# Message passing over 200,000 edges: rows of x @ W1[:64] gathered from a node table, both tables computed among the first twelve groups, 54 node updates

## The chip, the cores and the metric

The kernel runs on one core of one Trainium2 chip. The metric is the device time of one execution, in microseconds (us). A span is the time from the first to the last instruction of a profiled execution.

## The reference, cut to what matters

```python
# x: (12500, 64) nodes; src, dst: (200000,) with dst sorted; edge: (200000, 32)
msg_in = concatenate([x[src], x[dst], edge], axis=-1)          # 160 columns
messages = relu(msg_in @ mW1 + mb1) @ mW2 + mb2                # mW1 (160,128), mW2 (128,64)
aggregated = segment_sum(messages, dst, num_segments=12500)
upd_in = concatenate([x, aggregated], axis=-1)
out = layernorm(x + relu(upd_in @ uW1 + ub1) @ uW2 + ub2)      # per node, 64 columns
```

`src` is random, `dst` is sorted and dense at low nodes (nodes go as the square of a uniform number), so an early group of edges covers few nodes and a late one many.

## The kernel before, in words

The edges stand in 1563 tiles of 128. Eight tiles are a group, called `s` (`SUB`, 196 groups); sixteen are a supergroup `g` (`SUP`, 98). All work is written in a fixed order (`tc.manual_schedule()`), so each engine executes its instructions in the order of the loop over `s` at the end; a queue never overtakes.

For one group:

- `gather` (L148): POOL issues one indirect DMA for each tile; each brings 128 rows of x (64 columns, 256 bytes) chosen by `src`. Groups are gathered five ahead (`AHEAD`) into seven buffers.
- `transpose` (L268) turns pairs of tiles on PE, and ACT copies the result to `xt` (L272).
- `hidden` sums in PSUM the product of `xt` with W1[:64] (L290) and the product of the operand `l` with `rhs` (L294). The operand `l` holds the edge features and a selection of one of 32 nodes (a window) per edge; `rhs` holds W1[128:] and, for each tile, the 32 rows of the destination table B = x @ W1[64:128] + b1 that the tile can meet. ACT applies the relu (L298).
- `collect` (L309, L310) multiplies the hidden rows with a selection of slots, and also counts edges; `aggregate` (L322) adds eight windows of 32 columns to `comb` on DVE, at column offsets read from `wint`.

For one supergroup: `load` has SP bring `l` (edge features L235, and relative destinations broadcast over 32 partitions L236) and sixteen windows of B (L243); `select` on DVE turns destinations into selections (L252, L254), ACT casts them (L258). One supergroup later a node update follows: `columns`, `update`, `residual` and `norm` compute 384 nodes (L335 to L373) and SP writes them.

Before the loop, x transposed is loaded into `comb` (L88), B is computed in 25 chunks of 512 nodes (L222, L224) and written to DRAM by ACT's queue (L225); destinations less their tile's first destination are computed in bulk (L162 to L197), written to DRAM (`drow`) and checked: where the edges do not fit windows, a general path after L410 runs instead; these inputs do not take it.

SP and ACT issue their own DMAs, and POOL issues the gathers. Each DMA of SP or ACT waits, besides for its data, for the landing of the eighth DMA before it on the two queues together, in program order.

Of the kernel before, what the change touches and what calls it, by code (L numbers as in the profile page):

```python
# [17 lines left out]
P = 128  # L18
# [15 lines left out]
PADDST = -100000  # L34
EK, SK = 0, DE
AHEAD = 5
NCH = 4
UB = 3
NCOL = (-(-N // P) + UB) * P
ONE = 32  # L40
# [3 lines left out]
def gnn_kernel(ctx: ExitStack, tc: tile.TileContext, xT, x, one, eT, e_rows, src, dst, dst_row, wrow,  # L44
               mW1, mb1, mW2, mb2, uW1, ub1, uW2, ub2, out):

# [20 lines left out]

    B = dram.tile([NPAD, DH], F32, name="tab_b")
    drow = dram.tile([1, EBULK], F32, name="drow")


    src_s = const.tile([P, NT], I32, name="src_s")
    nc.scalar.dma_start(src_s[:, :64], src[:, :64])
    nc.scalar.dma_start(src_s[:, 64:], src[:, 64:])
    wint = const.tile([1, NTP], I32, name="wint")
    nc.sync.dma_start(wint, wrow)


    BF = mybir.dt.bfloat16
    w1b = const.tile([P, DH], F32, name="w1b")  # L80
    nc.sync.dma_start(w1b[D:], mW1[D:2 * D, :])
    b1 = const.tile([P, DH], F32, name="b1")
    nc.sync.dma_start(b1, mb1.rearrange("(o f) -> o f", o=1).broadcast_to([P, DH]))

    comb = const.tile([P, 2, NCOL], F32, name="comb")
    XCH = 2048
    for c in range(0, NCOL, XCH):
        nc.sync.dma_start(comb[D:, 1, c:min(c + XCH, NCOL)], xT[:, c:min(c + XCH, NCOL)])  # L88
    rhs = [const.tile([P, SUP // 2, DH], F32, name=f"rhs{k}") for k in range(2)]
    w1a = const.tile([P, DH], F32, name="w1a")  # L90
    for o in (0, 64):
        nc.scalar.dma_start(w1a[o:o + D], mW1[0:D, :])
    w2 = const.tile([DH, D], F32, name="w2")
    nc.scalar.dma_start(w2, mW2)
    b2c = const.tile([D, 1], F32, name="b2c")
    nc.scalar.dma_start(b2c, mb2.rearrange("(f o) -> f o", o=1))
    u1a = const.tile([D, DH], F32, name="u1a")
    nc.scalar.dma_start(u1a, uW1[D:2 * D, :])

    uz = const.tile([P, DH], F32, name="uz")  # L100
    nc.vector.memset(uz[:D], 0.0)
    nc.scalar.dma_start(uz[D:], uW1[0:D, :])
    ub1_s = const.tile([DH, 1], F32, name="ub1_s")
    nc.scalar.dma_start(ub1_s, ub1.rearrange("(f o) -> f o", o=1))
    u2 = const.tile([DH, D], F32, name="u2")
    nc.scalar.dma_start(u2, uW2)

    ux = const.tile([P, D], F32, name="ux")
    nc.vector.memset(ux[:D], 0.0)
    nc.scalar.dma_start(ux[ONE:ONE + 1], ub2.rearrange("(o f) -> o f", o=1))  # L110
    for r in rhs:
        for o in (EK, EK + 64):
            nc.scalar.dma_start(r[o:o + DE], mW1[2 * D:, :].unsqueeze(1).broadcast_to([DE, SUP // 2, DH]))

    ident = const.tile([P, P], F32, name="ident")
    make_identity(nc, ident)
    nc.vector.tensor_copy(ux[D:], ident[D:, D:])
    eps = const.tile([P, 1], F32, name="eps")
    nc.vector.memset(eps, EPS)
    ones = const.tile([P, 1], F32, name="ones")  # L120
    nc.vector.memset(ones, 1.0)
    slot_i = const.tile([P, WIN], I32, name="slot_i")
    nc.gpsimd.iota(slot_i, pattern=[[1, WIN]], base=0, channel_multiplier=0)
    pidx_i = const.tile([P, 1], I32, name="pidx_i")
    nc.gpsimd.iota(pidx_i, pattern=[[0, 1]], base=-SK, channel_multiplier=1)
    nc.gpsimd.iota(pidx_i[64:], pattern=[[0, 1]], base=-SK, channel_multiplier=1)

    cpool = ctx.enter_context(tc.tile_pool(name="cpsum", bufs=1, space=bass.MemoryType.PSUM))
    cps = cpool.tile([P, WIN + 1], F32, name="cps")
    nc.vector.tensor_copy(cps[:, :WIN], slot_i)  # L130
    nc.vector.tensor_copy(cps[:, WIN:], pidx_i)
    slot, pidx = cps[:, :WIN], cps[:, WIN:]
    w2u = const.tile([DH, DH], F32, name="w2u")

    one0 = const.tile([P, P], BF, name="one0")
    nc.vector.memset(one0, 0.0)
    nc.vector.memset(one0[:, 0:1], 1.0)

    rows = ctx.enter_context(tc.tile_pool(name="rows", bufs=AHEAD + 2))
# [5 lines left out]
    def gather(s):  # L145
        a = rows.tile([P, SUB, D], F32, name="xg")
        for i, t in enumerate(tiles(s)):
            nc.gpsimd.indirect_dma_start(  # L148
                out=a[:, i, :], out_offset=None, in_=x[:, :],
                in_offset=bass.IndirectOffsetOnAxis(ap=src_s[:, t:t + 1], axis=0))  # L150
        xg[s] = a

    for s in range(min(AHEAD, NSUB)):
        gather(s)


    drc = const.tile([P, NT], F32, name="drc")
    flag_i = const.tile([1, 1], I32, name="flag_i")
    usup = const.tile([1, NSUP], I32, name="usup")
    with tc.tile_pool(name="bulk", bufs=1) as bulk:  # L160
        dall = bulk.tile([P, TPP, P], I32, name="dall")
        nc.sync.dma_start(dall.rearrange("p t e -> p (t e)"), dst_row.rearrange("o (p c) -> (o p) c", p=P))  # L162
        wbc = bulk.tile([P, NT], I32, name="wbc")
        nc.scalar.dma_start(wbc, wrow[:, :NT].broadcast_to([P, NT]))
        dst_s = bulk.tile([P, NT], I32, name="dst_s")
        nc.scalar.dma_start(dst_s, dst)
        drel = bulk.tile([P, TPP, P], F32, name="drel")
        nc.vector.tensor_tensor(drel, dall, dall[:, :, 0:1].broadcast_to([P, TPP, P]), op=ALU.subtract)
        nc.sync.dma_start(drow.rearrange("o (p c) -> (o p) c", p=P), drel.rearrange("p t e -> p (t e)"))
        nc.vector.tensor_tensor(drc, dst_s, wbc, op=ALU.subtract)  # L170

        far = bulk.tile([P, TPP * P], F32, name="far")
        nc.vector.tensor_scalar(far, drel.rearrange("p t e -> p (t e)"), (WIN - 1) / 2.0, None, op0=ALU.subtract)
        nc.vector.tensor_tensor(far, far, far, op=ALU.mult)
        nc.vector.tensor_scalar(far, far, WIN * WIN / 4.0, None, op0=ALU.is_gt)
        nfar = bulk.tile([P, 1], F32, name="nfar")
        nc.vector.tensor_reduce(nfar, far, AX.X, ALU.add)
        pf = psum.tile([1, 1], F32, name="pf", tag="pt", bufs=1)
        nc.tensor.matmul(pf, nfar, ones, start=True, stop=True)

        wf = bulk.tile([1, NT], F32, name="wf")
        nc.vector.tensor_copy(wf, wint[:, :NT])
        back = bulk.tile([1, NT], F32, name="back")
        nc.vector.tensor_tensor(back[:, 1:], wf[:, 1:], wf[:, :-1], op=ALU.is_lt)
        nc.vector.tensor_copy(back[:, 0:1], pf)
        nc.vector.memset(usup[:, 0:1], 0)
        nc.vector.tensor_copy(usup[:, 1:], wint.rearrange("o (g t) -> o g t", t=SUP)[:, 1:, 0])
        uf = bulk.tile([1, NSUP + 1], F32, name="uf")
        nc.vector.tensor_copy(uf[:, :NSUP], usup)
        nc.vector.memset(uf[:, NSUP:], float(N - WIN))  # L190
        gap = bulk.tile([1, NSUP], F32, name="gap")
        nc.vector.tensor_tensor(gap, uf[:, 1:], uf[:, :-1], op=ALU.subtract)
        nc.vector.tensor_scalar(gap, gap, float(UB * P - WIN), None, op0=ALU.is_gt)
        bad = bulk.tile([1, 2], F32, name="bad")
        nc.vector.tensor_reduce(bad[:, 0:1], back, AX.X, ALU.add)
        nc.vector.tensor_reduce(bad[:, 1:], gap, AX.X, ALU.add)
        nc.vector.tensor_scalar(flag_i, bad[:, 0:1], bad[:, 1:], float((-E) % P), op0=ALU.add, op1=ALU.subtract)  # L197


    with tc.tile_pool(name="sup", bufs=2) as sup, tc.tile_pool(name="work", bufs=2) as work:  # L200
        L, S, SB, xs, hs, pht = {}, {}, {}, {}, {}, {}


        nc.vector.memset(comb[:, 0], 0.0)
        nc.vector.memset(comb[:D, 1], 0.0)
        nc.sync.dma_start(comb[ONE:ONE + 1, 1, :], one)
        pw = psum.tile([D, DH], F32, name="pw", tag="pt", bufs=1)
        nc.tensor.transpose(pw, w2, ident)
        w2T = work.tile([D, DH], F32, name="w2T", bufs=1)
        nc.vector.tensor_copy(w2T, pw)  # L210
        pw2 = psum.tile([DH, DH], F32, name="pw2", tag="pt", bufs=1)
        nc.tensor.matmul(pw2, w2T, u1a, start=True, stop=True)
        nc.vector.tensor_copy(w2u, pw2)
        pw3 = psum.tile([1, DH], F32, name="pw3", tag="pt", bufs=1)
        nc.tensor.matmul(pw3, b2c, u1a, start=True, stop=True)
        nc.vector.tensor_copy(uz[0:1, :], pw3)
        Bv = B.rearrange("(c p) f -> p c f", p=P)
        for c in range(0, NB, NCH):
            n = min(NCH, NB - c)
            pb = psum.tile([P, NCH, DH], F32, name="pb", tag="pc")  # L220
            for i in range(n):
                nc.tensor.matmul(pb[:, i, :], comb[D:, 1, (c + i) * P:(c + i + 1) * P], w1b[D:], start=True, stop=True)  # L222
# [152 lines left out]
        with tc.manual_schedule():  # L375
# [3 lines left out]
            for s in range(NSUB):  # L379
                g, j = divmod(s, SUP // SUB)  # L380
                if s + AHEAD < NSUB:
                    gather(s + AHEAD)
# [185 lines left out]
```

## Time and profile before

| | us |
|---|---|
| runs of the kernel before | 2006.89 median of 3 (2006.82 to 2007.45) |
| profiled execution, own time | 2007.04 |
| profiled execution, span | 2005.3 |
| POOL busy | 1481.1 (74% of the span) |
| PE busy, PE weight load busy | 1576.4 (79%), 1367.2 (68%) |
| DVE busy, ACT busy | 868.8 (43%), 493.0 (25%) |
| granted TensorE clock, mean | 0.789 |

In a list of instructions the columns are start, duration, engine, line and operation, the written tile and what is read, and in square brackets the idle time of the engine ahead of it with what ended it; "issue" means that nothing the profile shows ended it. PE is the matrix engine's product, PEld its weight load. A line of the table of stretches gives the stretch, its length, busy time with the number of instructions of PE, PEld, DVE, ACT and POOL, then the granted clock, the busy share of the DMA engines and GB/s.

### The profile page before, as it was taken

The numbers are of one execution on the slowest core, as the hardware profiler recorded it, in microseconds if no ns is written. First come the engines' busy times: TensorE is split into PE (matmuls) and PEld (weight loads), VectorE is DVE, ScalarE is ACT, GpSimd is POOL, SyncE is SP. The second block draws the span as 40 slices with busy tenths as digits, with TensorE's granted clock in tenths as the row PEclk, the third lists the DMA queues.
The fourth block names the chain that finished last, engine by engine and source line by source line (L and its number), as shares of the span: only waits on it lengthen the run. The fifth ranks groups of instructions, "written<-read, shape, count | busy, mean of one in ns | idle before, by whom it ended". The sixth has DMA issues, their size and how long they took to land.

```text
span 2005.3 us, 39767 instructions
## 1 busy us (share of the span) xinstructions
PE 1576.4 (79%) x12127; PEld 1367.2 (68%) x12127; DVE 868.8 (43%) x2894; ACT 493.0 (25%) x788; POOL 1481.1 (74%) x1572
## 2 busy tenths in 40 slices
PE   1999878877787778877778778778787877788787
PEld 0888766766676667666667667667676766677675
DVE  7356534343434343434443444344434444343443
ACT  0033322222222222222222222222222222222221
POOL 7767777777777777777777777777777777777771
PEclk9999777788777777777877787777777777877776
DMA  7634333333333333333332333333333333333330
GB/s 189 166 90 98 88 76 66 78 66 77 70 74 73 72 70 73 73 71 76 68 75 68 76 68 76 67 77 67 77 67 77 67 78 68 75 68 75 67 77 17
DMA packets 243690, 155.35 MB, mean 77 GB/s; under 512 B 96900, under 2 KB 211108, under 8 KB 243093
## 3 DMA queue, kind: packets, MB, share of 16 engines
q1 hardware_dynamic: 178020, 91.92, 18.7%
q0 software_dynamic: 50016, 51.32, 13.6%
q10 hardware_dynamic: 15442, 9.55, 1.8%
q8 instruction: 101, 1.65, 0.3%
q14 instruction: 111, 0.91, 0.2%
HBM read 135.65 MB, written 16.91 MB: 76 GB/s over the span
## 4 chain that ended last, share of the span: by engine, by line
POOL 44%; issue 20%; PE 18%; DMA 15%; SPq 1%; DVE 1%; POOLq 0%; ACT 0%; ACTq 0%; DVEq 0%
POOL xg L148 44%; DMA xg<-in_x,src_s 13%; PE ph L309 4%; PE pc L290 3%; PE pc L294 3%; PE pu L342 2%; PE pb L222 2%; PE pt L268 1%; PE pu L343 1%; DMA dall<-in_dst_row 1%; SPq L243 1%; PE py L353 1%; PE py L354 0%; DMA comb<-in_xT 0%; DMA rhs<-in_mW 0%
## 5 line engine op out<-in xcount | busy, mean ns | idle before, releaser
L148 POOL DMA_INDIRECT xg<-in_x,src_s x1563 | 1480.1, 947 | 483.8 <-issue 436.4
L322 DVE TENSOR_TENSOR comb<-comb,ph 128x64 f32 x1563 | 346.5, 222 | 592.0 <-PE pt L268 378.0
L268 PE MATMUL pt<-ident,xg 128*128 128x128 f32 x781 | 204.4, 324 | 360.8 <-DMA xg<-in_x,src_s 358.4
L290 PE MATMUL pc<-w1a,xt 64*128 64x128 f32 x3126 | 463.3, 381 | 1.5
L294 PE MATMUL pc<-rhs,l 64*128 64x128 f32 x3126 | 441.5, 366 | 7.8 <-issue 4.6
L309 PEld LDWEIGHTS ph<-sel,h 128*128 128x128 f32 x3126 | 401.3, 204 | 28.5 <-issue 4.5
L268 PEld LDWEIGHTS pt<-ident,xg 128*128 128x128 f32 x781 | 113.7, 156 | 425.3 <-issue 355.3
L309 PE MATMUL ph<-sel,h 128*128 128x32 f32 x3126 | 399.0, 284 | 0.1
L290 PEld LDWEIGHTS pc<-w1a,xt 64*128 64x128 f32 x3126 | 365.1, 275 | 37.7 <-issue 29.1
L294 PEld LDWEIGHTS pc<-rhs,l 64*128 64x128 f32 x3126 | 373.8, 279 | 9.7 <-issue 4.8
L298 ACT ACTIVATE h<-pc 128x1024 f32<-128x1024 f32 (+1 forms) x197 | 200.0, 1016 | 474.8 <-PE pc L294 421.3
L272 ACT COPY xt<-pt 128x512 f32<-128x512 f32 x196 | 114.3, 583 | 744.8 <-PE pt L268 732.2
L358 DVE BATCH_NORM_STATS2 st<-py 128x6 f32<-128x64 f32 x294 | 48.5, 221 | 470.7 <-PE py L354 452.7
L252 DVE TENSOR_TENSOR l<-l,cps 32x1024 f32<-32x1024 f32 x196 | 239.2, 1220 | 27.3 <-DMA l<-drow 20.9
L353 PE MATMUL py<-ux,xw 128*128 128x64 f32 x588 | 136.3, 319 | 0.7 <-ACT hTu L345 0.7
L354 PE MATMUL py<-u,hTu 128*128 128x64 f32 x588 | 129.1, 306 | 0.0
L342 PE MATMUL pu<-comb,w2u 128*128 x196 | 122.4, 716 | 7.3 <-DVE o L371 7.3
L353 PEld LDWEIGHTS py<-ux,xw 128*128 128x128 f32 x588 | 105.4, 224 | 17.2 <-issue 8.2
L354 PEld LDWEIGHTS py<-u,hTu 128*128 128x128 f32 x588 | 104.8, 223 | 0.0
L343 PE MATMUL pu<-xw,uz 128*128 128x384 f32 x196 | 85.8, 521 | 0.0
L371 DVE TENSOR_SCALAR o<-py,mv,rs 128x64 f32<-128x64 f32 x294 | 83.1, 338 | 3.6
L343 PEld LDWEIGHTS pu<-xw,uz 128*128 128x128 f32 x196 | 46.4, 237 | 40.0 <-issue 25.4
(67 smaller groups left out, 594.5 us busy)
## 6 DMA issues: line engine op xcount, KB each, us to landing
l<-in_eT SPq DMA_DIRECT2D x196, 128.0 KB
l<-drow SPq DMA_DIRECT2D x196, 128.0 KB
xg<-in_x,src_s POOLq DMA_INDIRECT x1563
rhs<-tab_b SPq DMA_DIRECT2D x1563, 16.0 KB
out<-o SPq DMA_DIRECT2D x98, 96.0 KB
tab_b<-tb ACTq DMA_DIRECT2D x24, 256.0 KB
comb<-in_xT SPq DMA_DIRECT2D x6, 512.0 KB
dall<-in_dst_row SPq DMA_DIRECT2D x1, 832.0 KB
```

What stands on the lines that cost most here:

```text
L148: nc.gpsimd.indirect_dma_start(out=a[:, i, :], out_offset=None, in_=x[:, :], in_offset=bass.IndirectOffsetOnAxis(ap=src_s[:, t:t + 1], axi ...
L252: nc.vector.tensor_tensor(m, m, pidx[q:q + WIN].broadcast_to([WIN, SUP // 2 * P]), op=ALU.is_equal)
L268: nc.tensor.transpose(pt[:, k, :], a[:, 2 * k:2 * k + 2].rearrange("p k d -> p (k d)"), ident)
L290: nc.tensor.matmul(pc[:, b, k, :], xt[q:q + 64, k, :], w1a[q:q + 64], start=True, stop=False)
L294: nc.tensor.matmul(pc[:, b, k, :], L[g][q:q + 64, m, :], rhs[g % 2][q:q + 64, m, :], start=False, stop=True)
L298: nc.scalar.activation(h[:, b, m], pc[:, b, m], AF.Relu)
L309: nc.tensor.matmul(ph[:, i, 0, :], h[:, i % 2, i // 2, :], S[g][:, k0 + i, :], start=True, stop=True)
L322: nc.vector.tensor_tensor(to, to, ph[:, i], op=ALU.add)
L342: nc.tensor.matmul(pu, w2u, comb[:, 0, bass.ds(u, UB * P)], start=True, stop=False)
L343: nc.tensor.matmul(pu, uz, xw, start=False, stop=True)
L353: nc.tensor.matmul(py[:, i], xw[:, i * P:(i + 1) * P], ux, start=True, stop=False)
L354: nc.tensor.matmul(py[:, i], hT[:, i * P:(i + 1) * P], u2, start=False, stop=True)
```

## The change

A second node table A = x @ W1[:64] is computed beside B and written to DRAM. Groups 0 to 11 (`XG`) still gather rows of x, all 96 gathers at the front of POOL's queue, and go through PE; from group 12 on the gather reads rows of A (128 columns, 512 bytes), and DVE adds them to the PSUM product of the operands, after which ACT's relu runs in place. The row buffers are six, each of twice the size. The 25 chunks of both tables are three ahead of the loop and the rest between steps 1 and 9, two or three a step (`TS` is 10). Six supergroups read B from a separate small copy `B0` of its first 1024 rows. The relative destinations come straight from `dst_row` and are compared with a node number; the checks and the weights of the updates move to steps 10 and 12. Node updates are made when about 320 nodes have gathered: 54 in place of 98.

```diff
-AHEAD = 5
+ROWB = 6
+XG = 2 * ROWB
 NCH = 4
+EARLY = 2 * NCH * P
+GE = XG // 2
+TS = 10
...
     def gather(s):
-        a = rows.tile([P, SUB, D], F32, name="xg")
+        if s >= XG or s % 2 == 0:
+            buf = rows.tile([P, SUB, DH], F32, name="xg")
+        else:
+            buf = xg[s - 1][0]
+        d = DH if s >= XG else D
...
             nc.gpsimd.indirect_dma_start(
-                out=a[:, i, :], out_offset=None, in_=x[:, :],
+                out=a[:, i, :], out_offset=None, in_=A[:, :] if s >= XG else x[:, :],
...
+        def select(g):
+            nt = min(SUP, NT - g * SUP)
+            l = L[g]
+            c = WIN + SUP // 2 * (g % 2)
+            node = cps[:, c:c + SUP // 2]
+            nc.vector.tensor_scalar(node, wh[:, g * SUP // 2:(g + 1) * SUP // 2], pidx, None, op0=ALU.add)
+            for r in ([slice(0, P)] if g > 2 else [slice(SK, SK + WIN), slice(64 + SK, 64 + SK + WIN)]):
+                nc.vector.tensor_tensor(l[r], l[r].bitcast(I32),
+                                        node[r].unsqueeze(2).broadcast_to([r.stop - r.start, SUP // 2, P]),
+                                        op=ALU.is_equal)
...
+        def edge_part(s):
...
+                nc.tensor.matmul(pc[:, b, k, :], L[g][q:q + 64, m, :], rhs[g % 2][q:q + 64, m, :],
+                                 start=s >= XG or k == 0, stop=s >= XG)
...
+        def node_part(s):
...
+            if s < XG:
+                xt = xs.pop(s)
...
+                    nc.tensor.matmul(pc[:, b, k, :], xt[q:q + 64, k, :], w1a[q:q + 64], start=False,
+                                     stop=i + 2 >= n)
+                nc.scalar.activation(h, pc, AF.Relu)
+            else:
+                a = xg.pop(s)[1].rearrange("p (k b) f -> p b k f", b=2)
+                for b, m in parts(n):
+                    nc.vector.tensor_tensor(h[:, b, m], pc[:, b, m], a[:, b, m], op=ALU.add)
+                    nc.scalar.activation(h[:, b, m], h[:, b, m], AF.Relu)
...
+        def xload(c):
+            e = min(c + XCH, NCOL)
+            nc.sync.dma_start(comb[ONE:, 1, c:e], x1T[:, c:e])
+        def relative(a, b):
+            wbc = work.tile([P, WCH], I32, name="wbc", tag="tb")
+            nc.sync.dma_start(dst_s[:, a:b], dst[:, a:b])
+            nc.sync.dma_start(wbc[:, :b - a], wrow[:, a:b].broadcast_to([P, b - a]))
+            nc.vector.tensor_tensor(drc[:, a:b], dst_s[:, a:b], wbc[:, :b - a], op=ALU.subtract)
...
+        def table(c):
+            n = min(NCH, NB - c)
+            xl = xls.pop(c)
+            pb = psum.tile([P, 2, NCH, DH], F32, name="pb", tag="pc")
+            for i in range(n):
+                o = (c + i) * P
+                nc.tensor.matmul(pb[:, 0, i, :], xl[:, i * P:(i + 1) * P], w1a[:D], start=True, stop=True)
+                nc.tensor.matmul(pb[:, 1, i, :], comb[D:, 1, o:o + P], w1b[D:], start=True, stop=True)
+            if c + 2 * NCH < NB:
+                xlower(c + 2 * NCH)
+            tb = work.tile([P, 2, NCH, DH], F32, name="tb")
+            nc.vector.tensor_tensor(tb[:, 1, :n], pb[:, 1, :n], b1.unsqueeze(1).broadcast_to([P, n, DH]), op=ALU.add)
+            if c * P < EARLY:
+                nc.sync.dma_start(B0v[:, c:c + n, :], tb[:, 1, :n])
+            nc.sync.dma_start(Bv[:, c:c + n, :], tb[:, 1, :n])
+            nc.scalar.copy(tb[:, 0, :n], pb[:, 0, :n])
+            nc.scalar.dma_start(Av[:, c:c + n, :], tb[:, 0, :n])
...
+        for s in range(XG):
+            gather(s)
...
+        table(chunks.pop(0))
+        table(chunks.pop(0))
+        nc.vector.memset(comb[:, 0], 0.0)
+        nc.scalar.copy(comb[:ONE, 1], zero1[:ONE].broadcast_to([ONE, NCOL]))
+        table(chunks.pop(0))
...
+        for s in range(last + 3):
+            g, j = divmod(s, SUP // SUB)
+            free = 0 if s < TS else XG + (s + 1) // 2 if s < XG else s + ROWB - 1
+            while gathered < min(free, NSUB):
+                gather(gathered)
+                gathered += 1
+            if s - 2 in due:
+                norm(due[s - 2])
+            if j == 0 and g + 1 < NSUP:
+                windows(g + 1)
+            if s < XG:
+                node_part(s)
+            if s in due and s < last:
+                columns(due[s])
+            if 1 <= s <= NSUB:
+                collect(s - 1)
+                aggregate(s - 1)
+            if j == 0 and g + 1 < NSUP:
+                select(g + 1)
+                load(g + 1)
+                counts(g + 1)
+            if j == 1 and g + 2 < NSUP:
+                loadd(g + 2)
+            while chunks and chunks[0] < NB * (s + 1) / TS:
+                table(chunks.pop(0))
+            if s + 1 < NSUB:
+                if s + 1 < XG:
+                    transpose(s + 1)
+                edge_part(s + 1)
+            if s == NSUB:
+                columns(K - 1)
+            if s in due:
+                update(due[s], "pt" if s == last else "pu")
+            if s - 1 in due:
+                residual(due[s - 1], "pt" if s - 1 == last else "pu")
+            if XG <= s < NSUB:
+                node_part(s)
+            rest(s)
```

In `rest`, steps 1 and 2 call `relative` for the remaining columns, step 10 loads the weights of the updates, and step 12 prepares them and makes the checks. `windows` is the loop over B's windows of the old `load`, `loadd` loads the destinations, and `load` the edge features. `xlower` has ACT load 512 columns of x transposed, two chunks ahead.

## The prediction

> **What bounds the kernel now.** I read the page's chain first, then the costliest groups, then the list of POOL's instructions in order of time.
>
> ```profile
> POOL 44%; issue 20%; PE 18%; DMA 15%; SPq 1%; DVE 1%; POOLq 0%; ACT 0%; ACTq 0%; DVEq 0%
> L148 POOL DMA_INDIRECT xg<-in_x,src_s x1563 | 1480.1, 947 | 483.8 <-issue 436.4
> ```
>
> PE has the larger busy share (79%), but the chain names POOL's gathers and the "issue" time between them. The list of POOL's instructions shows why:
>
> ```profile
> 95.73 0.94 POOL L148 DMA_INDIRECT xg<-in_x,src_s  x1 [0.30 <-issue]
> 96.98 0.94 POOL L148 DMA_INDIRECT xg<-in_x,src_s  x1 [0.30 <-issue]
> 104.42 0.94 POOL L148 DMA_INDIRECT xg<-in_x,src_s  x1 [6.50 <-PE pt L268]
> 105.66 0.94 POOL L148 DMA_INDIRECT xg<-in_x,src_s  x1 [0.30 <-issue]
> ...
> 1964.60 0.94 POOL L148 DMA_INDIRECT xg<-in_x,src_s  x1 [0.30 <-issue]
> ```
>
> From the 73rd gather (104.42) to the 1563rd (1964.60) there are 1490 steps in 1860.18 us, 1.2484 each, without one gap above the usual 0.30. POOL is the bound by itself: eight gathers are 9.99 us, and all other engines follow. The span is start 2.83, gathers, and a tail of 39.8 us after the last one (1965.5 to 2005.3). POOL loses little elsewhere: 6.2 us waiting for a buffer at 98, and some slowed gathers:
>
> ```profile
> 41.55 2.71 POOL L148 DMA_INDIRECT xg<-in_x,src_s  x1 [0.30 <-issue]
> ```
>
> and on DVE at that time:
>
> ```profile
> 41.21 1.87 DVE L174 TENSOR_TENSOR far<-far 128x1664 f32<-128x1664 f32 x1
> ```
>
> Five gathers beside DVE's bulk work at 15 to 44 us took 1.47, 1.61, 2.39, 1.63 and 2.71 instead of 0.94: 5.1 us lost.
>
> **The change part by part.** *PE work removed*: 733 of 781 transposes, 3030 of 3126 records of L290, 44 of 98 updates. About 840 us of PE record time (435 + 191 + 212, from the groups) goes, and some 90 us come for the tables. On the path this is worth nothing: POOL's 1563 gathers remain, at the same pace, and hide it.
>
> *Gathers of 512 bytes*: the trace has only 256-byte rows. POOL's 0.94 covers issuing 128 rows whatever their width; the number of rows stays. I take 0. From below it can't gain, as the rows are as many; from above, twice the bytes at twice the issue time would be +1467 × 0.94 = 1379 us, which I hold far-fetched, but +20 ns a gather would be +29 us. Landing hides: the DMA engines are 0.33 busy in the steady part.
>
> *DVE's add*, 184 times 128x1024: nearest row is L252 with as many columns and one PSUM operand, 1.22 us: 225 us, less half of L252's 239 us since one compare does two. Does it slow POOL? [...] If the add counted, 184 × 1.2 = +221 us. But it reads one operand from PSUM, as L322 does, and the gathers beside L322's 1563 adds took 0.94. I take 0. New two-SBUF work is only `relative` (1563 columns in three parts, 1.8 us by L170) in place of the bulk: about 1.5 us lost instead of 5.1, a gain of 3.6.
>
> *The loop of a late step*: with DVE's order, add(s) 1.2, relu 1.0, collect 2.3, aggregate 2.0, then add(s+1); plus select 2.1 and statistics 0.75 in even steps, norm 1.05 in odd ones: 9.6 and 7.8 with waits of about 0.1, mean 8.7 against POOL's 9.99. Hidden, with 1.3 us a step in hand. The checks and weights at steps 10 to 12 cost DVE about 7 us once; six row buffers (60 us) absorb it. The A rows' buffers are freed by the add some 45 us before they are wanted.
>
> *The tail*: at present a PE backlog (collect 3.46 us at the lowered clock, three updates) follows the last gather. Afterwards, from the last gather's end: landing 1.5 (2.45 from a gather's start), add of group 194 already done, its collect and aggregate to 4.3, add and relu of 195 to 5.4, one update's products to 6.1, collect and aggregate to 7.9, columns 0.5, products, relu, residual, statistics, norm to 15, write 3.8 (2001.45 to 2005.3): 19 at full clock, 23.5 at the lowered one. I take 20.5, a gain of 19.2.
>
> *Moved work at no cost*: `load` now follows `select` on SP, since the compare covers all 128 partitions; SP's edge loads wait for DVE there, with destination loads and B writes behind, and the next edge product waits for them. In the steady part SP uses about 10.5 of 20 us a pair (windows 8.5, edge loads 0.9, destinations 0.9), so DVE's lateness has 9 us of cover; without it each us shows in every second step. Ten weight loads move from the front to ACT at step 10, where ACT has most of a step free. Destinations come directly, without the 832 KB trip through `drow`, which only the front notices.
>
> *What it adds to the path*: gather 97 reads A and so waits until all of A has landed. POOL comes to it at 2.83 + 96 × 1.2484 + 1.5 = 124. Everything after is fixed: from A's landing, 1466 × 1.2484 + 0.94 = 1831.1, then 20.5. So span = A + 1851.6, and the change breaks even at A = 153.7. All depends on when A is ready.
>
> (a) The first edge product. B0's two chunks are written behind x transposed in SP's queue. The table of stretches shows the DMA's limit (share 1.03, 252 GB/s):
>
> ```profile
> 20.00:30.00 10.00, 0.00 (x0) 0.00 (x0) 9.15 (x1) 0.00 (x0) 7.56 (x9) 1.00 1.03 252
> ```
>
> The list of instructions shows when DVE got a load queued behind x transposed, and what sixteen window loads take; SP's waits show one of ACT's loads holding SP:
>
> ```profile
> 36.60 1.89 DVE L168 TENSOR_TENSOR drel<-dall 128x1664 f32<-128x1664 int32 x1 [4.92 <-DMA dall<-in_dst_row]
> ...
> 108.12 7.82 SPq L243 DMA_DIRECT2D rhs<-tab_b  x16
> ```
>
> ```profile
> SPq L88 <- DMA w1a<-in_mW: 5.7, 1, 5.7
> ```
>
> Some 8 MB had moved by 36.6 (the stretches' GB/s times their length); now about 7 MB stand there (x transposed 3.4, `src` 0.8, `rhs` 0.5, the gathers 0.9, columns of x and first tables 1.5), so 32 us. x transposed now has 65 rows instead of 64. [...] The trace shows 64 rows only (first chunk 2.43 to 10.04). [...] Then B0's second chunk lands at 39. The sixteen window loads are 8 us (7.82 to 9.20) when nothing holds them, but each SP or ACT load waits for the eighth before it (the row of L88 waiting for ACT's w1a shows that wait), and one of them waits for A's third chunk, written after ACT's zero copy of 12928 columns (11 us by L298's 1.02 per 1024). Windows end at 53, edge features land, first product 57. Bounds: 48 without that wait, 62.
>
> (b) Steps 0 and 1: products, copy, collect 2.3, aggregate 2.0, two table adds 1.4, with the next transposes and products 2 and hand-overs 1: to 68 (0.9 for eight products, from 1.8 for L290 and L294 together at full clock; collect is L309's 1.9 and L310's 0.3).
>
> (c) A pair of steps with five chunks. B's writes move from ACT's queue, where they had no neighbour, to SP's, where they stand behind the windows and edge loads of an even step: windows 8.5, edge loads 0.9, so the first B write is issued at 9.8. Behind it in SP's queue stand the other B writes and the next destinations. At that moment 0.26 MB of edge features, 0.5 MB of B, 0.5 MB of A and x are under way: 1.3 MB at 252 GB/s is 5 us, plus 1.4 to be seen (the last B write before was issued by 93.9, 0.4 of it is transfer, and SP went on at 95.8): 16. Only then is one of the two `tb` buffers free for the third chunk. DVE's add and ACT's copy of it wait for that, and behind the copy on ACT stands the next group's `xt`, for which PE waits: table copy 0.6, issue 0.45, `xt` copy 0.6, node product 0.9, collect 2.3, aggregate 2.0, the odd step's two adds 1.4: 24.3 a pair. Bounds: 20, the gathers' pace (in the trace a B write alone freed its buffer in about 2.2), and 28, if PE works at its lowered clock (L309's sixteen took 3.46 us at 1983, 1.9 at 1010).
>
> (d) Steps 2 and 3: a pair plus about 10, since `relative` takes a `tb` buffer, waits for its write, loads 0.5 MB twice and holds DVE: to 102.5. Three more pairs of 24.3: to 175.4. The last write's landing adds 1.5 and the estimates are no finer than that: I take A = 175.
>
> Sum: 51 of new wait, less 6.2 (the old buffer wait), 3.6 and 19.2: +22 on 2005.3, or directly 175 + 1851.6 = 2026.6. The profiled execution took 1.7 more than its span (2007.04) and stands 0.15 above the median of the runs: 2028.
>
> **The rivals.** *Tables keep the gathers' pace*: if SP's windows overlap the table writes and a pair takes 20 us or less from a start near 45, A is ready at 124 to 145. For it: PE needs about 7 us a step (transposes 0.6, two halves of products 1.8, collect 2.2, two and a half chunks 2.2 if their two 64-row halves overlap as L290's do), and writing B alone went at 1.7 us a chunk in 64 to 94. Against: there SP's queue held nothing else. Price: A = 130 gives 1981.6 + 1.6 = 1983; it decides below A = 153.7. *The late step's loop bounds*: if PE keeps the lowered clock, collect at 3.46 makes the loop 10.2, 0.2 × 184 = +40 beyond the forecast: 2068. Against: PE's load halves, and where PE was little busy the granted clock was 1.00 (stretch 20 to 30). *A 512-byte gather costs POOL 20 ns*: +29, 2057. *A later still*: pairs of 28 and a start at 62 give about 191 to 195, 2044 to 2048. That fewer updates do little is sure: they lie off the path.
>
> **How the numbers follow.** A measurement tells about 0.2%, 4 us, from no change, so same is A from 149.5 to 157.5. Forecast mechanism with A above 157.5: 0.66; near break-even: 0.06; tables keep pace: 0.14; loop bound 0.06; dearer gather 0.05; later A still 0.03. Faster 0.14, same 0.06, slower 0.80. The range takes A from 147 to 198, 2000 to 2052, leaving out most of the fast rival and the loop.
>
> **What would show it.** Right: POOL's list has one gap of 40 to 60 us at the 97th gather, ended by a DMA of tab_a, then 1.25 a gather to the end; table adds wait for tab_b writes; the tail near 20; granted clock up. Wrong: no such gap (the first rival), gathers longer than 0.94 after it, or gaps waiting for DVE later on.

## The result, and the profile after

The changed kernel takes 2091.05 us (median of four runs, 2089.09 to 2094.06), the kernel before 2007.03 in the same session: a ratio of 1.042, 95% interval 1.0402 to 1.0438. The forecast was slower, 2028, with a range up to 2052. The sign is right; the loss is 84 us where 21 was forecast. The profiled execution of after took 2094.06 with a span of 2092.1, against 2005.3 before.

The chain and the gathers' group, from the page of after (the first line is the chain's shares by engine):

```profile
PE 35%; POOL 20%; issue 15%; DVE 12%; DMA 10%; ACT 7%; SPq 1%; DVEq 1%; ACTq 0%; POOLq 0%
L153 POOL DMA_INDIRECT xg<-tab_a,src_s x1467 | 1384.1, 944 | 534.2 <-issue 409.7
```

A gather of 512 bytes costs POOL what one of 256 did: 944 ns on average, where before has 947. But PE, 18% of the chain before, now has 35%. POOL's list, around the 97th gather and at the end:

```profile
121.96 0.94 POOL L153 DMA_INDIRECT xg<-in_x,src_s  x1 [0.30 <-issue]
210.15 0.94 POOL L153 DMA_INDIRECT xg<-tab_a,src_s  x1 [87.25 <-DMA tab_a<-tb]
211.39 0.94 POOL L153 DMA_INDIRECT xg<-tab_a,src_s  x1 [0.30 <-issue]
...
2040.27 0.94 POOL L153 DMA_INDIRECT xg<-tab_a,src_s  x1 [0.30 <-issue]
```

The one gap that was forecast is there, ended by table A's last write, but it is 87.2 us and not 51. After it 1466 gathers follow at 1.2484 without a stop, and the last ends at 2041.2. The tail from there is 50.9 us, where before had 39.8 and the forecast 20.5. So the miss of 66 us in the span has two parts: A lands at 210 in place of 175 (35), and the tail is 30 longer than forecast.

The second part has a companion in the clock. The same stretch of the steady part, before and then after (columns as in the table of stretches; the third number from the end is the granted clock of PE, the TensorE):

```profile
1300.00:1900.00 600.00, 481.38 (x3678) 417.11 (x3677) 250.38 (x876) 150.53 (x241) 453.36 (x482) 0.76 0.33 72
```

```profile
1300.00:1900.00 600.00, 455.98 (x2363) 387.60 (x2362) 277.62 (x888) 112.52 (x172) 453.67 (x481) 0.57 0.37 97
```

PE executes 2363 records in place of 3678 and is nevertheless busy for 456 us in place of 481. The clock fell from 0.76 to 0.57, and over the whole run a record of the collection took 378 ns in place of 284. What PE waits for in that stretch (total, number of waits, longest), before and then after:

```profile
PE pt L268 <- DMA xg<-in_x,src_s: 117.5, 92, 3.1
PE ph L271 <- ACT h L259: 136.6, 58, 3.5
```

Before, PE waited in shorter pieces for gathered rows, 1.3 us each on average. Now it stands ahead of each collection, 2.4 us on average, until DVE has added the gathered rows to the edge product and ACT has applied the relu.

### The profile page after: what moved, and what is told of

Read it like the earlier page. It is cut to its first block, busy times and chain, and to the rows that moved or that the text cites. A ratio compares the mean times of both kernels' runs of the same rounds, so it can differ in the third digit from the quotient of the medians.

```text
span 2092.1 us, 31836 instructions
## 1 busy us (share of the span) xinstructions
PE 1440.7 (69%) x7951; PEld 1244.7 (59%) x7951; DVE 889.3 (43%) x2650; ACT 364.8 (17%) x497; POOL 1476.3 (71%) x1572
## 3 DMA queue, kind: packets, MB, share of 16 engines
q1 hardware_dynamic: 175380, 94.79, 16.6%
## 4 chain that ended last, share of the span: by engine, by line
PE 35%; POOL 20%; issue 15%; DVE 12%; DMA 10%; ACT 7%; SPq 1%; DVEq 1%; ACTq 0%; POOLq 0%
POOL xg L153 20%; PE ph L271 19%; DVE comb L283 6%; DMA xg<-tab_a,src_s 6%; ACT h L259 6%; PE pc L238 4%; PE pu L299 3%; DVE h L258 3%; PE py L310 3%; PE py L311 2%; PE pu L300 2%; DMA tab_a<-tb 1%; PE pb L391 1%; DVE st L315 1%; DMA tab_b<-tb 1%
## 5 line engine op out<-in xcount | busy, mean ns | idle before, releaser
L153 POOL DMA_INDIRECT xg<-tab_a,src_s x1467 | 1384.1, 944 | 534.2 <-issue 409.7
L271 PE MATMUL ph<-sel,h 128*128 128x32 f32 x3126 | 643.9, 378 | 506.3 <-ACT h L259 503.7
L271 PEld LDWEIGHTS ph<-sel,h 128*128 128x128 f32 x3126 | 619.7, 303 | 587.4 <-ACT h L259 584.5
L259 ACT ACTIVATE h<-h 128x1024 f32<-128x1024 f32 (+1 forms) x185 | 193.4, 1046 | 403.3 <-DVE h L258 332.6
L258 DVE TENSOR_TENSOR h<-pc,xg 128x1024 f32<-128x1024 f32 (+1 forms) x185 | 224.4, 1213 | 86.2 <-DMA xg<-tab_a,src_s 74.3
L192 ACT CAST selb<-sel 128x512 bf16<-128x512 f32 x98 | 60.4, 616 | 702.3 <-DVE sel L184 680.0
L180 DVE TENSOR_TENSOR l<-l,cps 128x1024 f32<-128x1024 int32 (+1 forms) x101 | 123.3, 1221 | 3.7 <-DVE cps L178 0.4
L153 POOL DMA_INDIRECT xg<-in_x,src_s x96 | 91.1, 949 | 30.1 <-issue 29.0
L311 PE MATMUL py<-u,hTu 128*128 128x64 f32 x324 | 102.8, 421 | 0.0
L310 PEld LDWEIGHTS py<-ux,xw 128*128 128x128 f32 x324 | 86.0, 325 | 13.5 <-issue 11.7
L311 PEld LDWEIGHTS py<-u,hTu 128*128 128x128 f32 x324 | 88.5, 333 | 0.0
L269 PE MATMUL ph<-selb,one 128*128 128x256 bf16 x196 | 72.9, 372 | 15.3 <-DVE cps L178 7.5
L184 DVE TENSOR_TENSOR sel<-cps,drc 128x512 f32<-128x512 f32 x98 | 66.9, 682 | 0.1
```

The source lines that it names most:

```text
L153: nc.gpsimd.indirect_dma_start(out=a[:, i, :], out_offset=None, in_=A[:, :] if s >= XG else x[:, :], in_offset=bass.IndirectOffsetOnAxis(a ...
L180: nc.vector.tensor_tensor(l[r], l[r].bitcast(I32), node[r].unsqueeze(2).broadcast_to([r.stop - r.start, SUP // 2, P]), op=ALU.is_equal)
L258: nc.vector.tensor_tensor(h[:, b, m], pc[:, b, m], a[:, b, m], op=ALU.add)
L259: nc.scalar.activation(h[:, b, m], h[:, b, m], AF.Relu)
L269: nc.tensor.matmul(ph[:, :n, 1, :], one0, SB[g][:, k0:k0 + n, :], start=True, stop=True)
L271: nc.tensor.matmul(ph[:, i, 0, :], h[:, i % 2, i // 2, :], S[g][:, k0 + i, :], start=True, stop=True)
```

## The experiments

Theory: two losses that don't depend on each other. First, table A lands late since a pair of steps with five chunks takes 32 us and not 24. Second, with 1300 fewer PE records in such a stretch the pauses are longer, the clock falls, the loop of a late step takes longer than eight gathers, and the row sums (DVE's adds of gathered rows to products, L258) fall behind the gathers, which shows as the tail. Rivals: one loss only, the long stop, which would also explain the clock; or a tail that comes from VectorE's new additions.

**A chip on which the loads of SyncE (SP) are slower.** On one chip the kernel before takes 2454.9 us. Four edits of the changed kernel ran there, twice each.

(1) Gathers that need no table: from group 12 on, 512-byte rows of the edge features' array are gathered instead of A, so what is added is not x @ W1[:64].

```diff
-in_=A[:, :] if s >= XG else x[:, :],
+in_=e_rows.rearrange("(a b) f -> a (b f)", b=DH // DE) if s >= XG else x[:, :],
```

> The changed kernel, except that from group 12 on the 512-byte rows are gathered from the edge features, read as rows of 128 columns, which are there from the start; both tables are computed as before, so the node part of the later groups is left out of the result. Theory 1 (the wait for the last write of A is all that holds POOL): the gap of 87 us at gather 97 goes, gathers end at 1955, the tail stays 51, about 2006 us. Theory 2 (the twelve early steps are late too, and with them the row buffers): groups 12 to 16 are gathered at once, but group 17 waits until the transposes of groups 10 and 11 at about 208, against 174 when POOL comes to it, so 40 to 50 us of wait come back in another place: about 2045 to 2055. Theory 3 (512-byte rows cost POOL more): gathers of more than 0.94 us; the trace of the changed kernel already shows 944 ns.

(2) All table chunks ahead of the loop.

```diff
-        table(chunks.pop(0))
-        table(chunks.pop(0))
         nc.vector.memset(comb[:, 0], 0.0)
         nc.scalar.copy(comb[:ONE, 1], zero1[:ONE].broadcast_to([ONE, NCOL]))
-        table(chunks.pop(0))
+        while chunks:
+            table(chunks.pop(0))
```

> The changed kernel with all 25 chunks of both tables ahead of the loop over groups in place of three, and the two zero fills before them. If the interleaving with windows, loads and aggregates is what makes the tables late, a chunk takes about 2.2 us (0.5 MB at 250 GB/s) from 33 us on, A is there at about 90, POOL finds it ready at 124, the first edge product comes at about 100, and a smaller wait of 10 to 20 us remains for row buffers, as the steps begin late: gathers end at about 1970, tail 51, about 2022 us. If the tables are slow by themselves (clock, DMA), A is ready no sooner than 150 and the time stays above 2050.

(3) The table products read their own copies of x transposed.

```diff
-xl = work.tile([D, NCH * P], F32, name="xl", bufs=2)
-nc.scalar.dma_start(xl, x1T[1:, c * P:(c + NCH) * P])
+xl = work.tile([P, NCH * P], F32, name="xl", bufs=2)
+for h in range(2):
+    nc.scalar.dma_start(xl[h * D:h * D + D], x1T[1:, c * P:(c + NCH) * P])
...
-nc.tensor.matmul(pb[:, 1, i, :], comb[D:, 1, o:o + P], w1b[D:], start=True, stop=True)
+nc.tensor.matmul(pb[:, 1, i, :], xl[D:, i * P:(i + 1) * P], w1b[D:], start=True, stop=True)
```

> The changed kernel with the tables' two products reading their own copies of x transposed (one more load a chunk), so that B's product no longer reads comb, which aggregate writes at columns known only at run time. If the product's wait for aggregate is a term of the pair of steps, a pair goes from 32 to about 28 us and A from 210 to about 193: about 2074 us. If the write behind the windows sets the pair alone, A stays at 205 to 210 and the time within 5 us of 2091.

(4) Two more products in each step from group 14 on, ahead of `node_part`; their result is not used.

```diff
+if XG + 2 <= s < NSUB - 1:
+    spin = psum.tile([P, SUB // 2, P], F32, name="spin", tag="pt", bufs=1)
+    for _ in range(2):
+        nc.tensor.matmul(spin.rearrange("p k e -> p (k e)"), ident,
+            rhs[(s + 1) // 2 % 2].rearrange("p k e -> p (k e)")[:, :SUB // 2 * P], start=True, stop=True)
```

> The changed kernel with two products of 128x512 without use added at the end of each step's PE work from group 14 on, where PE waits 2.8 us a step for the relu. Theory: PE's pauses lower its granted clock (0.56), which makes a late step longer than 9.99 us, and the lag of 24 us behind POOL and the slow tail come from that. Then the clock rises to 0.7 or more, the lag does not grow, the tail goes from 51 to about 30: about 2070 us. Rival: PE's own work is what is late, and the added 1.7 to 3.4 us a step make it worse: lag grows, over 2100 us.

They took 3229.8 and 3225.4 (1), 3210.8 and 3209.9 (2), 3258.1 and 3258.3 (3), 3252.4 and 3246.4 us (4). None of the expected times applies, for on that chip SP is held at its window loads. SP's list in the second run of (4):

```profile
1025.09 22.38 SPq L211 DMA_DIRECT2D rhs<-tab_b  x16
1050.31 0.79 SPq L199 DMA_DIRECT2D l<-in_eT  x2
1051.48 0.82 SPq L168 DMA_DIRECT2D l<-in_dst_row  x2
```

Sixteen window loads take 22.4 us, more than the 20 that POOL needs for a pair, where they took 9.5 in the pair of after that is shown further down. The chain of that profile gives 38% of its span to "another core or an unknown queue"; what makes the chip different was not found. These runs say nothing on the question, except for two things. The products of (4) lift the mean clock from about 0.54 to 0.66 there too. And in (1), which has no table to wait for, POOL stops all the same at the 97th and at each eighth gather after it up to the 137th, by the trace of its second run for "PE pt L219" (six waits, 137.8 us): the transposes of the first twelve groups, which free the row buffers, come late there. (1) was not run on another chip.

**Both losses taken away at once.** First the changed kernel itself on another chip, to have a base there:

> The changed kernel unaltered, as the base line of the chip on which the experiments run. On the chip of the first runs it took 2091 us beside 2007 of the kernel before. In the experiments so far the kernel before took 2455 us, as each of SP's loads of a window took 1.4 us in place of 0.5. If that is the chip, the changed kernel takes about 3230 us there: the same as with the wait for A taken out. If it is not, 2091 beside 2007.

Measured 2095.82 (one execution, as the next), with before at 2003.82 and a clock of 0.568. On the same chip the edits (2) and (4) together:

> The changed kernel with all 25 chunks of both tables ahead of the loop, and with two unused products of 128x512 at the end of each step's PE work from group 14 on. If the interleaved tables and the low clock of PE are the two causes: gathers end at about 1970, a tail of about 30, 2002 us where the kernel before takes 2007. If neither is: 2091. Where a window load of SP takes 1.4 us, SP is the bound and both theories give about 3210.

Measured 2028.27, clock 0.757: 67.6 us of the loss of 92.0 are gone, and 26 more than expected are left.

**One at a time.** Edits (2), (3) and (4) again, each alone, together on one chip with before at 2006.1.

> All 25 table chunks stand ahead of the first step and both zero fills ahead of them; everything else is as in the changed kernel. Two losses that don't depend on each other (late landing of table A, low TensorE clock): the 97th gather no longer waits for table A, but the steps of the first 12 groups start late, so the gathers stop for row buffers instead, some 50 to 60 us in all; the clock stays near 0.57 and the tail near 50: about 2055 us. Rival, one loss only (the clock is low because the long stop leaves TensorE idle at the start): the clock is near 0.75 and the tail near 25, about 2030 us.

Measured 2052.89 (ratio 1.0237, interval 1.0216 to 1.0257), clock 0.555: two losses. What POOL waits for:

```profile
POOL xg L153 <- PE pt L219: 31.2, 4, 8.8
POOL xg L153 <- DVE w2T L452: 12.1, 1, 12.1
```

There is no wait for table A: the 97th gather starts at 122.93. The second row is the 145th gather, at 225.28. It needs the buffer that the add of group 12 (223.80 to 225.01) frees; `w2T` is the copy just behind that add in DVE's list.

> Two products of 128x128 by 128x512 whose result is not used are added to each step from group 14 on; everything else is as in the changed kernel. Two independent losses: the stop at gather 97 stays at 80 to 90 us (it lies before the added products), the clock from group 14 on rises to 0.75, the row sums lag 2 to 4 us behind the gathers to the end, the tail is near 25 us: about 2065 us. Rival (the tail is long for another cause, such as VectorE's additions in the late steps): the tail stays near 50, about 2092 us.

Measured 2066.25 (1.0304, interval 1.0283 to 1.0324). The stop at gather 97 is still 84.6 us, and the steady stretch reads

```profile
1300.00:1900.00 600.00, 492.92 (x2683) 360.67 (x2684) 283.67 (x920) 116.61 (x178) 453.41 (x481) 0.79 0.37 97
```

More records than in after (2683), and fewer us of weight load (361 against 388). DVE's additions are all there, so they don't make the long tail; PE's pace does.

> Each chunk of x rows is loaded twice, to both halves of the partitions, and the table B products read that copy, not the node columns that the aggregation writes. If their wait for the aggregation of the same step set part of the 32 us of a pair of steps: a pair takes about 29 us, table A lands near 198 us in place of 210, the stop at gather 97 is about 75 us and the time about 2082 us. If TensorE's order of work sets it anyway (the products come when the collection is over, whether they wait or not): no change, 2092 to 2096 us.

Measured 2083.75 (1.0391, interval 1.037 to 1.0412); the stop is 80.4 us and the 97th gather starts at 203.99 in place of 210.15. The wait for the aggregation is worth 6 us of the 35, not more; each chunk of x is loaded twice here, so it may be worth somewhat more by itself.

The traces of these runs side by side (us; the stop is the time by which steps between gathers exceed 1.25; the tail runs from the last gather's end to the span's end):

| | stop | last gather ends | tail | clock |
|---|---|---|---|---|
| before | 11.7 | 1965.5 | 39.8 | 0.79 |
| after | 87.5 | 2041.2 | 50.9 | 0.56 |
| tables in front | 46.4 | 2000.2 | 51.2 | 0.56 |
| added products | 85.1 | 2039.0 | 23.6 | 0.75 |
| both | 48.1 | 2002.0 | 24.3 | 0.76 |
| own copies of x | 81.2 | 2035.7 | 48.2 | 0.56 |

Up to a few us the columns move one by one: the tables' place sets the stop and leaves the tail, the added products set the tail and leave the stop. In us, 38.2 and 24.8 below 2091.05 predict 2028.1 for both; 2028.27 was measured, on another chip. That the two agree so closely is luck: from the 2095.82 of the changed kernel on that chip the same sum gives 2032.8. That the two losses add up holds to some 5 us. With the tables in front the wait for A is gone, but a stop of 46 for row buffers takes its place: the first twelve steps start late, and a buffer of two groups of x comes free only when the second of its groups has been transposed.

**A version without either loss.** x rows up to group 48, tables over 24 steps, and the added products from group 50 (as in edit (4)). `GE`, half of `XG`, goes from 6 to 24 supergroups with it:

```diff
-XG = 2 * ROWB
+XG = 48
+TT = 24
...
-for s in range(XG):
+for s in range(2 * ROWB):
...
-free = 0 if s < TS else XG + (s + 1) // 2 if s < XG else s + ROWB - 1
+cap = ROWB + (s + 1) // 2
+free = s + ROWB - 1
+if s < XG:
+    free = min(2 * cap, XG) if s < TT else XG + max(cap - XG // 2, 0) if cap > XG // 2 else min(2 * cap, XG)
...
-while chunks and chunks[0] < NB * (s + 1) / TS:
+while chunks and chunks[0] < NB * (s + 1) / TT:
```

> Rows of x are gathered up to group 48 in place of 12, the table chunks are spread over 24 steps in place of 10, and the added products run from group 50. If the two losses are the whole of it, the gathers run almost without a stop (under 15 us in all, since the steps catch up while row buffers still hold two groups each), end near 1965 us, and the tail is near 25: about 1985 us, faster than the kernel before. If the steps can't catch up while they also transpose and multiply x rows, the stop comes at the change to table rows all the same, 40 to 60 us: about 2030 us.

Measured 1982.9 (1981.0 to 1983.88) against 2006.1: ratio 0.9885, interval 0.9868 to 0.9901: 1.1% faster than the kernel before. The stop is 0.7 us in all, and POOL's last gather

```profile
1953.76 0.94 POOL L154 DMA_INDIRECT xg<-tab_a,src_s  x1 [0.30 <-issue]
```

ends at 1954.7, 11 us earlier than before's. The tail is 27.3.

The same without the added products:

> As the run with x rows to group 48 and tables over 24 steps, but without the added products: is the later start enough, or does it need the higher clock? If the clock loss stands by itself: gathers almost without a stop, the clock near 0.57 from group 50 on, row sums that lag more and more in the last third and a tail near 45 to 50: about 2005 us, level with the kernel before. If the lag was a remnant of the early stop: a tail near 25 and about 1983 us.

Measured 2014.13 (2012.79 to 2018.21), ratio 1.0038, interval 1.0023 to 1.0053. The gathers end at 1954.9 here too, but the clock is 0.59 and the tail 61.5 where 45 to 50 was expected; the time is 9 us above the expected 2005. The row sums lag behind the end of their group's gather by 15.6 us at group 128 and by 42.5 at the last one. So the products are worth 31 us here, where after got 25 from them: in after the stop lets the row sums catch up, to a lag of about 2 us at group 36, and this version has no such stop.

Do the products alone help the kernel before? They were put ahead of its transposes, where PE waits for gathered rows:

```diff
+if 14 <= s < NSUB - 1:
+    spin = psum.tile([P, SUB // 2, P], F32, name="spin", tag="pt", bufs=1)
+    for _ in range(2):
+        nc.tensor.matmul(spin.rearrange("p k e -> p (k e)"), ident,
+            rhs[s // 2 % 2].rearrange("p k e -> p (k e)")[:, :SUB // 2 * P], start=True, stop=True)
 if s + 1 < NSUB:
     transpose(s + 1)
```

> The kernel before with two products of 128x128 by 128x512 added to each step from group 14 on, whose result is not used, ahead of the next group's transposes, where TensorE waits for the gathered rows. If the gain of the later start comes from the changed plan and not from the added products alone: the gathers go on at 1.2484 us and end at 1965, the clock goes up a little from 0.79, and the tail shortens by a few us: 2000 us or more. If the products alone do it: a tail near 25 and about 1990 us. If TensorE, busy for 79% here, becomes the bound: over 2010 us.

On two chips where before takes 2521.7 and 2447.9 the products made it slower, 2845.5 and 2731.3; the second one's chain has 31% for "another core or an unknown queue" again. Why was not found, and the gain of the products is shown only for chips on which before takes about 2006 us. On such a chip:

> Once more the kernel before with two products added to each step, in the hope of a chip on which the kernel before takes 2006 us. 2000 us or more if the products alone do little, 1990 us if they do it all, over 2010 us if TensorE becomes the bound.

Measured 2006.38 against 2006.12: ratio 1.0002, interval 0.9993 to 1.0011. The steady stretch:

```profile
1300.00:1900.00 600.00, 512.41 (x3907) 384.49 (x3907) 249.65 (x871) 148.56 (x240) 453.69 (x481) 0.93 0.31 72
```

The clock rises from 0.76 to 0.93 and the time doesn't move: POOL bounds that kernel, and only 2 us of its tail go (37.5 against 39.8). The gain of the version above therefore needs the change's plan and the products together: the plan alone gives +7 us (2014.13 against 2007.15), the products alone nothing, both -23.

## Why the prediction was right or wrong, point by point

**The bound and the gathers: right.** POOL's pace of 1.2484 us from A's landing to the end, 512-byte rows at no price, the gap at gather 97 and what ends it. DVE's add took 1.213 us against the 1.22 assumed, and the 331 gathers beside it took 0.940 to 0.956: this add, which reads PSUM, did not slow them. Beside the longest part of `relative`, which has two SBUF inputs, one gather took 1.31 (at 81.66); beside its two shorter parts the gathers took 0.94 and 0.95. What sets these apart was not shown.

**Steps (a), (b) and (d): right to a few us.** In (a), the 39 at which B0's second chunk was to land was the author's estimate; its write was issued at 38.33, and the first edge product, put at 57, started at 55.4. The last table add of step 1 stands at 70.5 (forecast 68), that of steps 2 and 3 at 107.95 (102.5). So of the 35 us by which A was late, 5.5 had passed here, 24.2 came in the three pairs of (c), and 5 behind the last add: it starts at 205.1, and POOL goes on at 210.15, where the prediction counted 1.5 for the landing and then left it out.

**Step (c), a pair with five chunks: wrong.** 24.3 was forecast; the last adds of the pairs stand at 107.95, 141.06, 173.19 and 205.1, so 33.1, 32.1 and 31.9. The upper bound of 28 was too low as well. SP's list of one pair:

```profile
140.08 2.11 SPq L398 DMA_DIRECT2D tab_b<-tb  x2
144.51 9.50 SPq L211 DMA_DIRECT2D rhs<-tab_b  x16
154.11 1.85 SPq L199 DMA_DIRECT2D l<-in_eT  x2
156.07 4.56 SPq L398 DMA_DIRECT2D tab_b<-tb  x3
```

and in its gap at 142.2, at line 206 of the kernel:

```profile
L206 SPq TENSOR_LOAD <-win x1: 2030/2030/2030, 142.2 to 142.2; - x1
```

DVE's list of the same pair:

```profile
159.54 0.69 DVE L395 TENSOR_TENSOR tb<-pb,b 128x512 f32<-128x512 f32 x1 [6.42 <-DMA tab_b<-tb]
167.62 2.02 DVE L283 TENSOR_TENSOR comb<-comb,ph 128x64 f32 x8 [7.40 <-PE ph L271]
171.86 0.69 DVE L395 TENSOR_TENSOR tb<-pb,b 128x512 f32<-128x512 f32 x1 [2.22 <-PE pb L391]
173.19 0.69 DVE L395 TENSOR_TENSOR tb<-pb,b 128x512 f32<-128x512 f32 x1 [0.64 <-ACT tb L399]
```

and PE's:

```profile
161.92 2.08 PE L252 MATMUL pc<-w1a,xt 64*128 64x128 f32 x16 [5.57 <-ACT xt L220]
164.13 3.46 PE L271 MATMUL ph<-sel,h 128*128 128x32 f32 x16
169.69 0.58 PE L391 MATMUL pb<-w1b,comb 64*128 64x128 f32 x1 [1.39 <-DVE comb L283]
```

The middle of the sum holds: from the first window load (144.51) to the third chunk's add (159.54) it is 15.0 us, and 16 was forecast, ended by a table B write as the prediction said. Both ends of the sum are short. Ahead of the windows SP is held by the odd step's last B write, which needs that step's last add, and then reads sixteen offsets for 2.03 us; the prediction let the windows begin with the pair and left that reading out: 2.8 us from the last add's end at 141.75. Behind the third add the prediction had 8.3 us, and 14.3 passed until 173.88: the node product took 2.08 in place of 0.9 and the collection 3.46 in place of 2.3, at a granted clock of 0.50 in place of the full one assumed (2.3 us together), and the table B products of the odd step read `comb`, which the aggregation has just written, so that from the end of the aggregation (169.64) to the end of the last add 4.2 us pass in place of 1.4. The first and the last of these are waits that the program's order shows; the order of the queues should have been walked around the whole pair, to where SP comes back to the windows. Of these terms only the read of `comb` was taken out by itself, by the copies of x: it is worth 6 us over all pairs. The others are read from the lists.

**PE's work removed at no price, and the tail of 20.5: wrong.** The step that failed is "on the path this is worth nothing", and with it "hidden, with 1.3 us a step in hand" and "granted clock up". The prediction took less work on PE for a higher clock; that the clock could fall wasn't weighed. In the runs fewer records and longer pauses went with 0.57, and two more products a step with 0.79. The length of single pauses does not tell the clock: the longest in the stretch from 1300 to 1900 is 3.5 in after, at 0.57, and 5.8 with the added products, at 0.79; two neighbouring steps late in after show pauses of 3.15 and 1.51 us. What goes with the clock in these 600 us is the sum of the pauses in PE's largest row of waits: 81.2 us at 0.93 (before with products), 97.4 at 0.79 (after with products), 117.5 at 0.76 (before), 136.6 at 0.57 (after). What ties the two was not shown. The rows with products, before and after:

```profile
PE pt L268 <- DMA xg<-in_x,src_s: 81.2, 57, 2.6
PE ph L271 <- ACT h L259: 97.4, 38, 5.8
```

The prediction's ground for a rising clock was the stretch from 20 to 30 us of before, at 1.00. That stretch has no PE instruction at all (x0), and the trace of before has no record of the clock ahead of 106 us, where the column then shows 1.00. PE's first products there, at 10.18, are in such a stretch too and took 417 ns each; in after the same products took 0.42 us where 0.50 is recorded (149.2 to 151.4) and 0.27 where 1.00 is (153.6 to 154.4).

PE's list of the two late steps (the bracket has the pause):

```profile
1881.22 3.62 PE L271 MATMUL ph<-sel,h 128*128 128x32 f32 x16 [3.15 <-ACT h L259]
1884.78 2.08 PE L238 MATMUL pc<-rhs,l 64*128 64x128 f32 x16
...
1891.39 2.29 PE L271 MATMUL ph<-sel,h 128*128 128x32 f32 x16 [1.51 <-ACT h L259]
```

and on DVE the row sums of these steps, with the statistics of a node update:

```profile
1878.80 1.23 DVE L258 TENSOR_TENSOR h<-pc,xg 128x1024 f32<-128x1024 f32 x1 [0.19 <-issue]
...
1887.12 1.23 DVE L258 TENSOR_TENSOR h<-pc,xg 128x1024 f32<-128x1024 f32 x1 [0.15 <-issue]
...
1898.47 0.49 DVE L315 BATCH_NORM_STATS2 st<-py 128x6 f32<-128x64 f32 x3 [0.75 <-PE py L311]
...
1899.38 1.22 DVE L258 TENSOR_TENSOR h<-pc,xg 128x1024 f32<-128x1024 f32 x1 [0.19 <-issue]
```

Two steps take 20.58 us, 10.29 each, against 9.99 of POOL. That is the rival "the late step's loop bounds", whose 10.2 was near; it was given 0.06 because the clock was expected to rise. It does not take the +40 that the rival counted, since it holds only in the last third: the lag of the row sums is about 2 us from group 36 to 124, then grows to 16 at 164 and 30 at the end.

Why only there? From group 124 on a node update falls in every pair of steps, before that in every second pair at most. DVE's statistics of the update wait for PE's products of L311, which stand behind the edge product, and the next row sum stands behind the statistics: the second of the two steps takes 12.26 us, the first 8.32. In the pairs in which the row sums run more than 3.5 us behind the gathers, so that the loop goes at its own pace, a pair with an update takes 20.6 us on average and one without 18.3 (35 and 21 pairs of the run with the tables in front; 20.6 and 18.3 in the version without added products too). POOL takes 19.97 for a pair. In the version with the later switch and the added products such pairs take 18.7 and 16.6 (4 and 8 pairs), both below POOL's. So at the low clock the updates, which the prediction held to lie off the path, are on it.

With the added products the lag stays between 1.6 and 5.2 us from group 36 on and the tail is 23.6, near the prediction's own 20.5 to 23.5. The tail's working assumed the add of group 194 done when the last gather ends. With the added products it is (first line; the last gather ends at 2038.97), in after it comes 22 us behind that end at 2041.2 (second line):

```profile
2036.93 1.22 DVE L258 TENSOR_TENSOR h<-pc,xg 128x1024 f32<-128x1024 f32 x1 [0.95 <-DMA xg<-tab_a,src_s]
2063.36 1.23 DVE L258 TENSOR_TENSOR h<-pc,xg 128x1024 f32<-128x1024 f32 x1 [0.19 <-issue]
```

So the tail's working was right for a loop that keeps up with POOL, and that assumption was wrong: 25 of the 27 us between the two tails are the lag (30.2 against 5.2 at the last group).

A count was off too, without weight for the result: the twelve groups that keep L290 have 192 of its records, so 2934 of 3126 went, not 3030.

**Break-even.** It was put at A = 153.7 with a tail of 20.5; with the tail of 50.9 it would have been at about 123, where POOL comes to gather 97 anyway. With that tail an earlier A could have brought the change level with before, not ahead of it.

## What to carry to other kernels

Work taken from an engine that is not the bound was not free of effect here (PE's granted clock went from 0.76 to 0.57): where a loop through several engines has little in hand against the bound (1.3 us of 9.99 was the estimate here), cost it also at the lower clock that the emptier engine may be granted, for its fullest step and not for the mean, and give that a real chance. Read a granted clock only where the engine works (the 1.00 from 20 to 30 us stood over no PE instruction). When part of a producer is moved in between other steps, walk its queue around one whole period, back to where it started, with the register reads and the reads of data that a neighbour has just written. And a wait that is taken away shows what stands behind it: without the wait for A, 46 us of waiting for row buffers took its place, until the switch to table rows was put later, where the row buffers (60 us) cover the lag of the steps (42 us at group 48).

## What the runs showed of the hardware that had not been expected

- TensorE's granted clock fell when it had less to do: 0.76 to 0.57 in the same 600 us, with 2363 records in place of 3678. Products whose results nobody reads brought it back to 0.79, and in the kernel before to 0.93.
- On three of the chips the kernel before took 2448 to 2522 us in place of 2006. On one of them a window load on SP, with its offset from a register, took 1.40 us in place of 0.5 to 0.6 (0.72 and 0.75 on the other two), and the changed kernel with its edits 3210 to 3258 us.
- Reading sixteen offsets into SP's registers took 0.97 us in the steady part of both kernels, but 2.0 to 3.1 in each of the last four readings of after while the tables were made (109.1, 142.2, 174.3 and 206.0). Why was not found.
